# Strassen's scheme for the two projections of a graph-attention layer (stage 0 of a two-layer kernel)

## The chip, the cores and the metric

The kernel runs on one core of one Trainium2 chip. The metric is the device time of one execution in microseconds (us). The five engines of the core are called by their names or by the profile's short forms: TensorE (PE, with its weight loads as PEld), VectorE (DVE), ScalarE (ACT), GpSimd (POOL) and SyncE (SP).

## The reference

Two graph-attention layers run one after the other on 4096 nodes with 512 features in fp32. Only the first layer's projections matter here:

```python
h = jnp.maximum(_layernorm(x, axis=-1), 0.0)      # [4096, 512]
node_att = jax.nn.softmax(h @ node_w, axis=0)     # one logit for each node
he = h @ edge_w                                   # [4096, 512] x [512, 512]
e = jnp.where(adj > 0, he @ he.T, NEG_BIG)
edge_att = jax.nn.softmax(e, axis=1)
support = h @ weight                              # [4096, 512] x [512, 512]
x = x + (adj * (node_att * edge_att)) @ support + bias
```

Stage 0 of the kernel computes the normalised and rectified h, the node logits, `support` (the tile `sup`), the transposed `he` (the tiles `he_t`), and stores x + bias for later. Everything after it (the scores, the attention sums, the second layer) is left as it is by the change.

## The kernel before

The nodes are handled in 32 tiles of 128 rows (t = 0 to 31) and in 8 blocks of 512 rows, four tiles each (b = 0 to 7). The order of all instructions in stage 0 is written out by hand: each engine runs its own queue in the order in which the code names the instructions, and waits on semaphores where data or a buffer is not ready.

What happens to a tile, with the helpers' lines in the kernel before:

- `fetch` (L130) loads 128 rows of x into one of 8 slots `xt`, on SP's queue.
- `stats` (L134) makes mean and variance on VectorE and the square root on ScalarE. `norm` (L142) makes the reciprocal and the shift on VectorE and then h on ScalarE (L149, or L151 for tiles 8 and up, which are written in an order of 32x32 squares).
- `logit` (L153) multiplies h by the node weights with a sum on VectorE (`acc_z`, L154); GpSimd adds the bias into a tile `xb` of its own, of which there is one (L157), and stores it on its own queue (L158).
- `turn` (L176) transposes h. The first 8 tiles go through TensorE (L188) and are copied out of PSUM by VectorE (L189). Later tiles are sent to memory in four pieces (`send`, L160, SP's queue, with the tile's logit), read back in another order (`pull`, L171, SP's queue) and turned in squares by VectorE (L181).

What happens to a block: `support` (L192) multiplies each turned tile by `ws`, in 4 accumulating matmuls of 512 columns into a tile `ps` (two PSUM buffers), which VectorE copies to `sup` (L198). `edges` (L200) makes each 128-row part of `he_t[b]` from `we` and the whole turned block, 4 matmuls of 512 columns into `pe` (two buffers), which ScalarE copies (L205). The loop is L248 to L254: for block b it does the four `edges`, with one `step` (L216) of block b+1 behind each, and then the four `support` of block b+1. A step names, in this order, the fetch of tile t+10 (t+7 early on), the norm and the send of tile t+4, the turn of tile t, the pull of tile t+2 and the stats of tile t+5.

Behind the last block come the maximum of all logits and the softmax over nodes (L257 to L269), alternating between VectorE, GpSimd and ScalarE. Stage 1 (from L289) begins with score tiles of 512, 384, 256 and 128 columns (L331) in six PSUM buffers; ScalarE copies each out (L334) and VectorE masks it and takes maxima (L336 to L344).

Of the kernel before, what the change touches and what calls it, by code (L numbers as in the profile page):

```python
# [8 lines left out]
FP = mybir.dt.float32  # L9
AF = mybir.ActivationFunctionType  # L10
ALU = mybir.AluOpType
AX = mybir.AxisListType
PSUM = bass.MemoryType.PSUM
DRAM = bass.MemoryType.DRAM

P = 128
# [12 lines left out]
def kernel(  # L29
# [15 lines left out]
    nc = tc.nc  # L45
    N, F = x.shape
# [4 lines left out]
    KC = F // P  # L51
    BL = 512
    NB = N // BL
    TB = BL // P
# [27 lines left out]
    sup = big.tile([P, NT, F], FP, name="sup")  # L82
    na = big.tile([P, NT], FP, name="na")
    s_n = big.tile([P, H, NT], FP, name="s_n")
    t_m = big.tile([P, H, NT], FP, name="t_m")
# [10 lines left out]
    he_t = []  # L96
# [3 lines left out]

    with tc.tile_pool(name="w0", bufs=1) as wp, tc.tile_pool(name="a0", bufs=2) as ap_, tc.tile_pool(
        name="a0s", bufs=8
    ) as sp, tc.tile_pool(name="a0p", bufs=2, space=PSUM) as pp, tc.manual_schedule():
        we = wp.tile([P, KC, F], FP, name="we")
        ws = wp.tile([P, KC, F], FP, name="ws")
        nw_b = wp.tile([P, F], FP, name="nw_b")
        nw = wp.tile([P, KC], FP, name="nw")
        bias_b = wp.tile([P, F], FP, name="bias_b")
        nc.sync.dma_start(nw, node_w)
        nc.scalar.dma_start(ws, weight.rearrange("(k p) f -> p k f", p=P))  # L110
        nc.scalar.dma_start(we, edge_w.rearrange("(k p) f -> p k f", p=P))
        nc.gpsimd.dma_start(bias_b, row_bcast(bias, F))

        pw = pp.tile([P, KC, P], FP, name="pt")
        for k in range(KC):
            nc.tensor.matmul(pw[:, k, :], nw[:, k:k + 1].to_broadcast([P, P]), ident, start=True, stop=True)
        nc.vector.tensor_copy(nw_b.rearrange("p (k q) -> p k q", k=KC), pw)
        lg = wp.tile([P, NT], FP, name="lg")
        xts, mvs, sds, hs, hts, hqs = {}, {}, {}, {}, {}, {}
        T0 = 2 * TB  # L120
        nw_s = mb_0

        def squares_of(h):

            return h.rearrange("p (c k q) -> p k c q", c=P // S, q=S)

        def columns_of(x_):
            return x_.rearrange("p (k c q) -> p k c q", k=KC, q=S)

        def fetch(t):  # L130
            xts[t] = sp.tile([P, F], FP, name="xt", bufs=8)
            nc.sync.dma_start(xts[t], x[t * P:(t + 1) * P, :])

        def stats(t):  # L134
            st = sp.tile([P, 6], FP, name="st")
            nc.vector.bn_stats(st, xts[t])
            mvs[t] = sp.tile([P, 2], FP, name="mv")
            nc.vector.bn_aggr(mvs[t], st)
            sds[t] = sp.tile([P, 1], FP, name="sd")
            nc.scalar.activation(sds[t], mvs[t][:, 1:2], AF.Sqrt, bias=eps)  # L140

        def norm(t):  # L142
            rs = sp.tile([P, 1], FP, name="rs")
            nc.vector.reciprocal(rs, sds.pop(t))
            mr = sp.tile([P, 1], FP, name="mr")
            nc.vector.scalar_tensor_tensor(mr, mvs.pop(t)[:, 0:1], -1.0, rs, op0=ALU.mult, op1=ALU.mult)
            hs[t] = sp.tile([P, F], FP, name="h", bufs=5)
            if t < T0:
                nc.scalar.activation(hs[t], xts[t], AF.Relu, bias=mr, scale=rs)  # L149
            else:  # L150
                nc.scalar.activation(squares_of(hs[t]), columns_of(xts[t]), AF.Relu, bias=mr, scale=rs)  # L151

        def logit(t, h):  # L153
            nc.vector.tensor_tensor_reduce(acc_z, h, nw_b if t < T0 else nw_s, 1.0, 0.0, ALU.mult, ALU.add,  # L154
                                           lg[:, t:t + 1])
            xb = sp.tile([P, F], FP, name="xb", bufs=1)
            nc.gpsimd.tensor_tensor(xb, xts.pop(t), bias_b, ALU.add)  # L157
            nc.gpsimd.dma_start(xb_d[t * P:(t + 1) * P, :], xb)  # L158

        def send(t):  # L160


            if t < T0:
                return
            h = hs.pop(t)
            to = h_d[t].rearrange("(c p) (a k q) -> a p c (k q)", p=S, k=KC, q=S)
            for a in range(P // S):
                nc.sync.dma_start(to[a], h[a * S:(a + 1) * S, :].rearrange("p (c f) -> p c f", c=P // S))
            logit(t, h)

        def pull(t):  # L171
            if t >= T0:
                hqs[t] = sp.tile([P, F], FP, name="hq", bufs=2)
                nc.sync.dma_start(hqs[t], h_d[t])

        def turn(t):  # L176
            b, j = divmod(t, TB)
            if j == 0:
                hts[b] = ap_.tile([P, KC, BL], FP, name="h_t")
            if t >= T0:  # L180
                nc.vector.transpose(  # L181
                    hts[b][:, :, j * P:(j + 1) * P].rearrange("p k (a q) -> p k a q", q=S),
                    hqs.pop(t).rearrange("p (a k q) -> p k a q", k=KC, q=S))
                return
            h = hs.pop(t)
            pt = pp.tile([P, KC, P], FP, name="pt")
            for k in range(KC):
                nc.tensor.transpose(pt[:, k, :], h[:, k * P:(k + 1) * P], ident)  # L188
            nc.vector.tensor_copy(hts[b][:, :, j * P:(j + 1) * P], pt)  # L189
            logit(t, h)  # L190

        def support(t):  # L192
            b, j = divmod(t, TB)
            ps = pp.tile([P, F], FP, name="ps")
            for k in range(KC):
                nc.tensor.matmul(ps, hts[b][:, k, j * P:(j + 1) * P], ws[:, k, :],  # L196
                                 start=(k == 0), stop=(k == KC - 1))
            nc.vector.tensor_copy(sup[:, t, :], ps)  # L198

        def edges(b, d):  # L200
            pe = pp.tile([P, BL], FP, name="pe")
            for k in range(KC):
                nc.tensor.matmul(pe, we[:, k, d * P:(d + 1) * P], hts[b][:, k, :],  # L203
                                 start=(k == 0), stop=(k == KC - 1))
            nc.scalar.copy(he_t[b][:, d, :], pe)  # L205

        done = {fetch: 0, stats: 0, norm: 0, send: 0, pull: 0}

        def upto(f, t):
            while done[f] < min(t + 1, NT):
                f(done[f])
                done[f] += 1

        def step(t):  # L216
            if t < NT:
                upto(fetch, t + 10 if t >= T0 else t + 7)
                upto(norm, t + 4)
                upto(send, t + 4)  # L220
                turn(t)
                upto(pull, t + 2)
                upto(stats, t + 5)

        upto(fetch, 7)
        upto(stats, 1)
        upto(norm, 0)
        upto(stats, 2)
        upto(norm, 1)
        turn(0)  # L230
        upto(stats, 3)
        upto(norm, 2)
        turn(1)
        support(0)
        upto(norm, 3)
        turn(2)
        support(1)
        upto(stats, 5)
        upto(norm, 4)
        turn(3)  # L240
        support(2)
        upto(norm, 5)
        support(3)
        upto(fetch, 9)
        upto(stats, 8)
        upto(norm, 7)
        nc.gpsimd.tensor_copy(squares_of(nw_s), columns_of(nw_b))
        for b in range(NB):  # L248
            for j in range(TB):
                edges(b, j)  # L250
                step((b + 1) * TB + j)
            if b + 1 < NB:
                for j in range(TB):
                    support((b + 1) * TB + j)  # L254


        m1 = sp.tile([P, 1], FP, name="m1")  # L257
        nc.vector.tensor_reduce(m1, lg, AX.X, ALU.max)
        m2 = sp.tile([P, 1], FP, name="m2")
        nc.gpsimd.partition_all_reduce(m2, m1, P, bass_isa.ReduceOp.max)  # L260
        m3 = sp.tile([P, 1], FP, name="m3")
        nc.vector.tensor_scalar(m3, m2, -1.0, None, ALU.mult)
        s1 = sp.tile([P, 1], FP, name="s1")
        nc.scalar.activation(na, lg, AF.Exp, bias=m3, accum_out=s1)
        s2 = sp.tile([P, 1], FP, name="s2")
        nc.gpsimd.partition_all_reduce(s2, s1, P, bass_isa.ReduceOp.add)
        s3 = sp.tile([P, 1], FP, name="s3")
        nc.vector.reciprocal(s3, s2)
        nc.vector.tensor_scalar(na, na, s3, None, ALU.mult)  # L269

# [18 lines left out]
    with tc.tile_pool(name="mx", bufs=1) as mxp, tc.tile_pool(name="b_a", bufs=6) as adjp, tc.tile_pool(  # L289
        name="b_e", bufs=4  # L290
    ) as esp, tc.tile_pool(name="b_m", bufs=2) as mkp, tc.tile_pool(name="b_s", bufs=2) as sp, tc.tile_pool(
        name="b_p", bufs=6, space=PSUM
# [56 lines left out]
        for n in range(-6, len(items)):  # L349
# [3 lines left out]
            if n >= 0:  # L353
                i, j, t = items[n]
# [9 lines left out]
    with tc.tile_pool(name="c_a", bufs=11) as adjp, tc.tile_pool(name="c_b", bufs=4) as ebp, tc.tile_pool(  # L364
        name="c_e", bufs=9
    ) as etp, tc.tile_pool(name="c_w", bufs=3) as wkp, tc.tile_pool(name="c_t", bufs=3) as atp, tc.tile_pool(
        name="c_m", bufs=2
    ) as mxp, tc.tile_pool(name="c_o", bufs=4) as iop, tc.tile_pool(name="c_s", bufs=2) as sp, tc.tile_pool(
        name="c_p", bufs=1, space=PSUM
# [754 lines left out]
```

## Time and profile before

| what | value |
|---|---|
| median of 3 runs | 2927.29 us (2926.97 to 2927.95) |
| the profiled execution: its own time | 2927.71 us |
| its span, first to last instruction | 2925.9 us |
| TensorE busy, share of the span | 2880.2 us, 98% |
| VectorE busy | 2539.2 us, 87% |
| ScalarE busy | 1314.6 us, 45% |
| GpSimd busy | 1418.0 us, 48% |
| mean granted TensorE clock | 0.995 |
| stage 0: first transpose to last edge matmul | 12.15 to 241.4 us |

How to read the views that follow. A row of the timeline has the start in us, the length in us, the engine, the line of the kernel, the operation, the tile written and the tiles read, the shape, and how many such instructions were merged. Square brackets hold the idle time of the engine just before, and what ended it. A row of the chain of work has start, length, engine, tile and line, and how many instructions. The length of a matmul row is modelled, and neighbouring matmuls overlap, so the distance between starts tells the pace. A matmul written in the code appears as two instructions (and two weight loads) in the trace.

### The profile page before, as it was taken

The numbers are of one execution on the slowest core, as the hardware profiler recorded it, in microseconds if no ns is written. First come the engines' busy times: TensorE is split into PE (matmuls) and PEld (weight loads), VectorE is DVE, ScalarE is ACT, GpSimd is POOL, SyncE is SP. The second block draws the span as 40 slices with busy tenths as digits, with TensorE's granted clock in tenths as the row PEclk, the third lists the DMA queues.
The fourth block names the chain that finished last, engine by engine and source line by source line (L and its number), as shares of the span: only waits on it lengthen the run. The fifth ranks groups of instructions, "written<-read, shape, count | busy, mean of one in ns | idle before, by whom it ended". The sixth has DMA issues, their size and how long they took to land.

```text
span 2925.9 us, 42903 instructions
## 1 busy us (share of the span) xinstructions
PE 2880.2 (98%) x14987; PEld 1127.2 (39%) x14987; DVE 2539.2 (87%) x3607; ACT 1314.6 (45%) x1798; POOL 1418.0 (48%) x1093
## 2 busy tenths in 40 slices
PE   8999999999999999999999989999999999999998
PEld 4444444444444444444444423322222322222222
DVE  5435777778898998988987789999999999999998
ACT  2221111111122222222221058888777787777786
POOL 3401111112434434444444776676767676767675
PEclk9999999999999999999999989999999999999999
DMA  5525666667877756756655259898989898989896
GB/s 180 176 79 192 224 220 220 228 225 184 201 176 189 204 151 193 195 163 187 196 168 154 69 150 238 236 244 235 242 237 237 239 237 241 233 243 229 218 230 171
DMA packets 517032, 587.66 MB, mean 201 GB/s; under 512 B 291832, under 2 KB 344088, under 8 KB 516816
## 3 DMA queue, kind: packets, MB, share of 16 engines
q1 hardware_dynamic: 460336, 410.90, 46.5%
q0 software_dynamic: 54464, 170.10, 26.1%
q10 hardware_dynamic: 2016, 3.93, 0.4%
q8 instruction: 117, 1.92, 0.3%
q14 instruction: 99, 0.81, 0.1%
HBM read 418.91 MB, written 73.60 MB: 168 GB/s over the span
## 4 chain that ended last, share of the span: by engine, by line
PE 79%; DVE 11%; ACT 4%; issue 4%; DMA 1%; SPq 1%; DVEq 0%; POOL 0%; ACTq 0%; POOLq 0%
PE po L481 27%; PE pv L895 19%; PE pe L331 15%; DVE pr L863 7%; PE dn L900 6%; PE po L592 4%; PE ps L196 3%; PE pe L203 3%; ACT e L827 2%; DVE pr L860 1%; PE pt L954 1%; DVE pt L442 1%; ACT rl L845 1%; DMA eb<-e_d 0%; ACT ex L817 0%
## 5 line engine op out<-in xcount | busy, mean ns | idle before, releaser
L895 PE MATMUL pv<-pr,sup 128*32 128x512 f32 x8192 | 1020.1, 594 | 8.5 <-POOL d_m L1066 5.6
L481 PE MATMUL po<-sup,at 128*128 128x512 f32 x2048 | 883.8, 594 | 7.2 <-DMA eb<-e_d 6.1
L872 POOL TENSOR_TENSOR acc<-acc,pr 128x1024 f32<-128x1024 f32 x240 | 574.0, 2391 | 310.0 <-DVE pr L863 309.4
L863 DVE SCALAR_TENSOR_TENSOR pr<-z,g_m,ex 128x1024 f32<-128x1024 f32 x512 | 630.1, 1270 | 0.0
L481 PEld LDWEIGHTS po<-sup,at 128*128 128x128 f32 x2048 | 388.5, 190 | 494.5 <-issue 454.8
L461 POOL TENSOR_TENSOR racc<-racc,ex 128x512 f32<-128x512 f32 x240 | 352.7, 1469 | 389.3 <-ACT ex L445 387.9
L895 PEld LDWEIGHTS pv<-pr,sup 128*32 128x32 f32 x8192 | 290.6, 110 | 607.3 <-issue 564.7
L445 ACT ACTIVATE ex<-d 128x512 f32<-128x512 f32 x256 | 160.5, 630 | 611.2 <-DVE d L443 605.9
L331 PE MATMUL pe<-he_t,he_t 128*128 128x512 f32 x896 | 386.4, 592 | 0.0
L817 ACT ACTIVATE ex<-e 128x1024 f32<-128x1024 f32 x256 | 263.3, 1028 | 240.9 <-DVE pr L863 239.7
L900 PE MATMUL dn<-pr,d_m 128*2 128x512 f32 x1984 | 343.6, 592 | 0.0
L863 DVE SCALAR_TENSOR_TENSOR pr<-z,g_m,e 128x1024 f32<-128x1024 f32 x256 | 327.8, 1281 | 0.0
L827 ACT ACTIVATE e<-e,ld_m 128x1024 f32<-128x1024 f32 x256 | 290.6, 1135 | 0.0
L860 DVE SCALAR_TENSOR_TENSOR pr<-rl,ngd_m,ex 128x1024 f32<-128x1024 f32 x223 | 283.2, 1270 | 2.1 <-ACT ex L817 1.6
L845 ACT ACTIVATE rl<-z,ngd_m,d_m 128x1024 f32<-128x1024 f32 x223 | 273.9, 1228 | 0.0
L335 POOL DMA_DIRECT2D e_d<-es x144 | 78.7, 546 | 364.5 <-ACT es L334 359.0
L331 PEld LDWEIGHTS pe<-he_t,he_t 128*128 128x128 f32 x896 | 169.2, 190 | 210.1 <-issue 190.8
L334 ACT COPY es<-pe 128x512 f32<-128x512 f32 (+2 forms) x144 | 79.3, 551 | 377.0 <-PE pe L331 377.0
L451 DVE TENSOR_TENSOR at<-ex,a 128x512 f32<-128x512 f32 x256 | 187.3, 732 | 64.6 <-ACT ex L445 38.8
L443 DVE TENSOR_TENSOR d<-pt,mk 128x512 f32<-128x512 f32 x256 | 177.0, 691 | 8.8
L336 DVE CUSTOM_DVE_ANT_0 mk<-pe,mk 128x512 f32<-128x512 f32 (+2 forms) x144 | 93.0, 646 | 98.8 <-ACT es L334 98.7
L878 POOL DMA_DIRECT2D acc<-pr x160 | 138.2, 863 | 5.8 <-DMA acc<-pr 2.8
(183 smaller groups left out, 2539.7 us busy)
## 6 DMA issues: line engine op xcount, KB each, us to landing
e<-in_adj_t_dram SPq DMA_DIRECT2D x256, 512.0 KB, 5.9
acc<-pr POOLq DMA_DIRECT2D x176, 512.0 KB, 5.7
a<-in_adj_t_dram SPq DMA_DIRECT2D x256, 256.0 KB, 4.0
ar<-in_adj_dram SPq DMA_DIRECT2D x120, 256.0 KB, 3.0
e_d<-es POOLq DMA_DIRECT2D x120, 256.0 KB, 3.0
eb<-e_d SPq DMA_DIRECT2D x456, 64.0 KB, 2.9
ac<-in_adj_t_dram SPq DMA_DIRECT2D x112, 256.0 KB, 3.6
et<-e_d SPq DMA_DIRECT2D x112, 256.0 KB, 4.8
```

Source lines behind the costliest of these rows:

```text
L331: nc.tensor.matmul(pe[:, :w], he_t[i][:, k, (t % TB) * P:(t % TB + 1) * P], he_t[j][:, k, BL - w:], start=(k == 0), stop=(k == KC - 1))
L451: nc.vector.tensor_tensor(w, e, aj.pop((b, m)), ALU.mult)
L461: nc.gpsimd.tensor_tensor(racc, racc, e, ALU.add)
L481: nc.tensor.matmul(po[j], w[:, j * P:(j + 1) * P], sup[:, m, :], start=(m == 0), stop=last)
L817: nc.scalar.activation(x_, ra.pop((i, m)), AF.Exp)
L827: nc.scalar.activation(x_, ra[i, m], AF.Exp, bias=ld_m[:, h // HG, m:m + 1])
L845: nc.scalar.activation(r, zs_[i, 0], AF.Relu, bias=ngd_m[:, h // HG, m:m + 1], scale=d_m[:, h, m:m + 1])
L860: nc.vector.scalar_tensor_tensor(w, rl.pop((i, m)), ngd_m[:, h // HG, m:m + 1], x_, op0=ALU.subtract, op1=ALU.mult)
L863: nc.vector.scalar_tensor_tensor(w, zs_[i, k], g_m[:, h + k, m:m + 1], e3.pop((i, m)) if k == 3 else x_, op0=ALU.max, op1=ALU.mult)
L872: nc.gpsimd.tensor_tensor(acc[i, 3], acc[i, 3], w, ALU.add)
L895: nc.tensor.matmul(v[c][q][r * D + c0:r * D + c0 + Q, :], va[:, m, g * HG + k, c0:c0 + Q], pr[i, m, k][:, q * BL:(q + 1) * BL], start=(m = ...
L900: nc.tensor.matmul(dn[r * Q:r * Q + w.shape[1], :], w, src[:, q * BL:(q + 1) * BL], **fl)
```

## The change

Only stage 0 is touched. For blocks 1 to 7 each of the two products (turned block times `ws`, and times `we`) is cut in quarters and made in Strassen's scheme, in Winograd's form with shared sums: seven products of quarters in place of eight. One product of quarters is 4 matmuls in the code, each of 256 columns, and its two halves fill one PSUM bank. Block 0 keeps `support` and `edges`.

- The weights' sums are made once: three tiles for each matrix on GpSimd ahead of block 0's edges (`weight_sums`), and one difference for each in place on VectorE behind block 0 (`last=True`).
- A block's four row sums are made on VectorE right behind the turn of its last tile (`row_sums`), three of them in a `he_t` tile not yet written (for block 7 in `xt` slots), one in place.
- The first product of a set is copied from PSUM by ScalarE; the others are added on VectorE, 7 additions a set, into `sup`, `he_t[b]` or a scratch tile (`parts_of`).
- All of stage 0's PSUM tiles share one name with 8 buffers.
- `xt` has 6 slots rather than 8 and h 4 buffers rather than 5; the bias is added in place in the `xt` slot, so the separate `xb` tile is gone.
- The steps follow the products numbered 3, 6, 9 and 11 of the block's 14. In a step the turn and the row sums come first, then norm, stats, send, fetch and pull. The turns of tiles 6 and 7 come together.

The diff, cut to its core:

```diff
-        name="a0s", bufs=8
-    ) as sp, tc.tile_pool(name="a0p", bufs=2, space=PSUM) as pp, tc.manual_schedule():
+        name="a0s", bufs=8
+    ) as sp, tc.tile_pool(name="a0p", bufs=8, space=PSUM) as pp, tc.manual_schedule():
...
+        XT = 6
...
-            xts[t] = sp.tile([P, F], FP, name="xt", bufs=8)
+            xts[t] = sp.tile([P, F], FP, name="xt", bufs=XT)
...
-            hs[t] = sp.tile([P, F], FP, name="h", bufs=5)
+            hs[t] = sp.tile([P, F], FP, name="h", bufs=4)
...
-            xb = sp.tile([P, F], FP, name="xb", bufs=1)
-            nc.gpsimd.tensor_tensor(xb, xts.pop(t), bias_b, ALU.add)
+            xb = xts.pop(t)
+            nc.gpsimd.tensor_tensor(xb, xb, bias_b, ALU.add)
             nc.gpsimd.dma_start(xb_d[t * P:(t + 1) * P, :], xb)
...
+        def weight_sums(key, w, last=False):
+            B11, B12, B21, B22 = w[:, LO, L], w[:, LO, R], w[:, HI, L], w[:, HI, R]
+            if last:
+                nc.vector.tensor_tensor(B12, B12, B11, ALU.subtract)
+                Ts[key].update({1: B11, 2: B21, 3: B22, 5: B12})
+                return
+            t2, t3 = (wp.tile([P, KC // 2, BL // 2], FP, name=f"{key}t{n}") for n in (2, 3))
+            nc.gpsimd.tensor_tensor(t3, B22, B12, ALU.subtract)
+            nc.gpsimd.tensor_tensor(t2, t3, B11, ALU.add)
+            Ts[key] = {6: t2, 7: t3}
+            if key == "s":
+                t4 = Ts[key][4] = wp.tile([P, KC // 2, BL // 2], FP, name="st4")
+                nc.gpsimd.tensor_tensor(t4, B21, t2, ALU.subtract)
+            else:
+                t4 = Ts[key][4] = [s.rearrange("p h t -> p (h t)") for s in (s_n, t_m)]
+                for k in range(KC // 2):
+                    nc.gpsimd.tensor_tensor(t4[k], B21[:, k, :], t2[:, k, :], ALU.subtract)
+
+        def row_sums(b):
...
+            nc.vector.tensor_tensor(s1, A21, A22, ALU.add)
+            nc.vector.tensor_tensor(s2, s1, A11, ALU.subtract)
+            nc.vector.tensor_tensor(A21, A11, A21, ALU.subtract)
+            nc.vector.tensor_tensor(s4, A12, s2, ALU.subtract)
+            As[b] = {1: A11, 2: A12, 3: s4, 4: A22, 5: s1, 6: s2, 7: A21}
+
+        def product(key, b, n):
+            acc = pp.tile([P, 2, BL // 2], FP, name="bank")
+            A, B = As[b][n], Ts[key][n]
+            for j in range(2):
+                js = slice(j * P, (j + 1) * P)
+                for k in range(KC // 2):
+                    Bk = B[k] if isinstance(B, list) else B[:, k, :]
+                    w, m = (A[:, k, js], Bk) if key == "s" else (Bk[:, js], A[:, k, :])
+                    nc.tensor.matmul(acc[:, j, :], w, m, start=(k == 0), stop=(k == KC // 2 - 1))
+            return acc
...
+            nc.scalar.copy(u, product(key, b, 1))
+            yield
+            add(C[0, 0], u, product(key, b, 2))
+            yield
+            add(u, u, product(key, b, 6))
+            yield
+            add(C[0, 1], u, product(key, b, 5))
+            yield
+            bank = product(key, b, 7)
+            add(C[1, 1], C[0, 1], bank)
+            add(C[1, 0], u, bank)
+            yield
+            add(C[0, 1], C[0, 1], product(key, b, 3))
+            yield
+            add(C[1, 0], C[1, 0], product(key, b, 4))
+            yield
...
-                upto(fetch, t + 10 if t >= T0 else t + 7)
+                if t == T0 - 2:
+                    turn(t)
+                    turn(t + 1)
+                elif t != T0 - 1:
+                    turn(t)
+                if t % TB == TB - 1:
+                    row_sums(t // TB)
                 upto(norm, t + 4)
+                upto(stats, t + 5)
                 upto(send, t + 4)
-                turn(t)
+                upto(fetch, t + 9 if t >= T0 else t + XT)
                 upto(pull, t + 2)
-                upto(stats, t + 5)
...
-        for b in range(NB):
-            for j in range(TB):
-                edges(b, j)
-                step((b + 1) * TB + j)
-            if b + 1 < NB:
-                for j in range(TB):
-                    support((b + 1) * TB + j)
+        weight_sums("s", ws)
+        weight_sums("e", we)
+        for j in range(TB):
+            edges(0, j)
+            step(TB + j)
+        weight_sums("s", ws, last=True)
+        weight_sums("e", we, last=True)
+        for b in range(1, NB):
+            n = 0
+            for key in "se":
+                for _ in parts_of(key, b):
+                    n += 1
+                    if n in (3, 6, 9, 11):
+                        step((b + 1) * TB + (3, 6, 9, 11).index(n))
```

## The prediction

> **What bounds the kernel now.** I read the page first, then stage 0 (from 0 to 242 us) in the chain of work, the timeline and the table by form. The page says which engine the span belongs to:
>
> ```profile
> PE 2880.2 (98%) x14987; PEld 1127.2 (39%) x14987; DVE 2539.2 (87%) x3607; ACT 1314.6 (45%) x1798; POOL 1418.0 (48%) x1093
> ```
>
> An average over the span doesn't price one stage, so the end of the chain inside stage 0 (start, length, work):
>
> ```profile
> 186.42 13.73 PE ps L196 x32
> 200.16 13.73 PE pe L203 x32
> 213.89 13.73 PE ps L196 x32
> 227.62 13.75 PE pe L203 x32
> 241.39 0.59 ACT he_t L205
> 241.99 0.04 issue
> ```
>
> TensorE alone carries it: each block of 512 nodes is 13.73 us of support and 13.73 us of edges, with nothing between. A 4-deep accumulation of 16 matmuls is recorded as 32 instructions, so one record of 512 columns takes 13.73/32 = 0.429 us. The stage after it is TensorE's as well (the L331 records follow at the same 0.43 us), so TensorE time taken out of stage 0 comes off the end.
>
> Two places are not pure work. TensorE waits once for 2.2 us and, at 137.6 us, once for 0.5 us, both times for a support copy that VectorE reaches late:
>
> ```profile
> 54.89 7.13 PE L196 MATMUL ps<-ws,h_t 128*128 128x512 f32 x16 [2.23 <-DVE sup L198]
> ```
>
> Why VectorE is late is visible in pairs of rows of the timeline:
>
> ```profile
> 129.56 1.26 POOL L157 TENSOR_TENSOR xb<-xt,bias_b 128x512 f32<-128x512 f32 x1 [2.64 <-DMA xb_d<-xb]
> 129.68 1.69 DVE L154 CUSTOM_DVE_ANT_0 acc_z<-h,mb 128x512 f32<-128x512 f32 x1 [0.93 <-ACT h L151]
> ...
> 26.10 0.68 DVE L154 CUSTOM_DVE_ANT_0 acc_z<-h,nw_b 128x512 f32<-128x512 f32 x1
> 26.16 1.75 POOL L157 TENSOR_TENSOR xb<-xt,bias_b 128x512 f32<-128x512 f32 x1 [2.85 <-DMA xb_d<-xb]
> ```
>
> Who starts first takes its usual time (1.26 us, 0.68 us); the other is held until it ends.
>
> Last, what a 256-column matmul costs beside its weight load, from the evictions behind score tiles of 384, 256 and 128 columns:
>
> ```profile
> 248.35 0.48 ACT L334 COPY es<-pe 128x384 f32<-128x384 f32 x1 [1.95 <-PE pe L331]
> 250.07 0.37 ACT L334 COPY es<-pe 128x256 f32<-128x256 f32 x1 [1.25 <-PE pe L331]
> 250.97 0.27 ACT L334 COPY es<-pe 128x128 f32<-128x128 f32 x1 [0.52 <-PE pe L331]
> ```
>
> Eight records of 256 columns lie between the first two: 1.72/8 = 0.215 us each, half of 0.429. The 0.190 us weight load stays hidden even there.
>
> **What the Trainium skill says.** *TensorE: Matmul & The Clock Gate*, Back-to-back issue gap: in a stream of weight loads and matmuls both together set the spacing. The trace agrees, with 0.215 us against 0.190 us: at 256 columns the margin is only 25 ns. *SBUF — State Buffer*, Who interferes with whom: VectorE and GpSimd share a port pair that is locked for a whole instruction; a VectorE instruction with two SBUF inputs contends with a GpSimd one that reads SBUF, one with at most one SBUF input doesn't. The pairs above agree with the first half; the second matters for the new additions (one PSUM input, one SBUF input), and no row with GpSimd adding beside them shows it. *PSUM — Partial Sum Buffer*, Specifications: 8 banks of 512 fp32 values, so a product of 2 x 256 fills one bank, and the change takes all 8.
>
> **Part by part.** *Matmuls, blocks 1 to 7.* Removed: 32 x 2 records of 0.429 us, 27.46 us a block. Added: 14 products x 8 records x 0.215 us = 24.08 us. Saved: 3.38 x 7 = 23.7 us, all on the path. Unknown: whether 0.215 us holds for other operands; from 0.2145 (half of 0.429) up to 0.24. I take 0.215.
>
> *The two old stalls.* Support no longer has two buffers of its own but shares 8 banks: 2.2 + 0.5 = 2.7 us more.
>
> *VectorE in a full block (1 to 5).* Start to start: a turned tile 0.63, statistics 0.69 + 0.10, reciprocal and product 0.30, logit 0.62: 2.34 us, four times, 9.4. The sup copies go. New: 14 additions from a bank, at 0.61 us (stage 1's additions from a bank, mean 0.69 us, start 0.60 apart) plus 0.1 where one reads the one before: 9.1. Row sums, 4 at 0.61 plus two such waits: 2.6. Wait for h, about 0.2 a tile since statistics now lie between: 0.8. Sum 21.9 us, under TensorE's 24.08. Bounds of a new operation: 0.60 to 0.75 us (strided results), which gives 21.7 to 24.4. VectorE needn't be on time to the product either: eight banks are 13.8 us of cover, and block b+1's first need of a row sum is its third product, 8.6 us after the step that makes it; turning and two sums take 1.9 us, an addition before it about 1: 5.7 us of slack. If that cover goes, every us of lateness costs one.
>
> *ScalarE.* 28 copies of 0.57 us go, 14 come; it is busy 52 of 241 us: nothing.
>
> *GpSimd.* Each xb addition is now in place, so it waits for h (ScalarE), the moment at which the logit starts too. By the rows above logit starts 0.03 to 0.08 us after h; GpSimd's instructions begin 0.1 to 0.3 us after what they wait for. So VectorE should win, and GpSimd be held (1.75 us), which costs nothing: 4 x (1.75 + 0.3 + 0.56) = 10.4 us of 24. If GpSimd wins, VectorE pays about 1.2 us a tile (rival 2). New weight sums: five of 128x512 and two halves at 1.26 to 1.75 us with 0.3 between, about 10 us, from 24 to 34 us, ahead of xb(4) on GpSimd's queue.
>
> *SP and the x tiles, where I expect a new stall.* There are 6 slots, not 8, and one is free only when its xb store has landed (median 3.0 us). So fetch(10) waits for xb(4): added at 34 to 35.3, store issued 35.6, landed 38.6; on SP it stands behind send(8), issued 38.8, landed (4.0 us) 42.8. VectorE's step 5 reaches stats(10) at 39.5 and waits 3.3 us. Fetch(11) waits for xb(5) and lands at 48.5, about when wanted; the logits of tiles 6 and 7 meet xb(6) and xb(7), 0.5 and 1.0 us; fetch(12), behind send(10), is issued at 51.0 and lands at 55.2. Step 7 makes block 1's second row sum by 51.3, then waits from 53 to 55.2 for stats(12), and behind that, the logit and this queue stand the last weight sums: ws is ready at 57.2. TensorE is through block 0 at 45.6 and wants the row sum after two products (49.0) and that weight sum after three: it waits 2.3 + 4.1 = 6.4 us. Bounds: none, if stores land a us sooner each and VectorE is never held, to 10 us if each link is 1 us later. I take 6.4. Later fetches run five tiles ahead and pulls have 8.6 us or more (landing 3.1 us, four sends and a fetch at 0.44 each before them): hidden.
>
> *The end of stage 0.* The logit maximum, the exponential and the release of stage 1's loads now stand behind VectorE's last addition rather than a support copy 13.7 us earlier. Before, TensorE's end to the first load was 3.4 us, with a table load of 1.28 us in it that no longer has to wait for the last copy; the new chain is longer by two hops. I make it equal, 0 to 2 us later. Stage 1's first six tiles, 15.4 us, need no release (bank 0 was freed 6 us early): nothing.
>
> **Sum.** 23.7 + 2.7 - 6.4 = 20.0 us. The profiled execution took 2927.71 us (span 2925.9 and 1.8 around it); 2927.71 - 20.0 = 2907.7. The runs' median is 0.4 us lower, so I say 2907.5. Change under 0.2% (5.9 us) can't be told from none here.
>
> **Rivals.** (1) No start-up stall: stores at startup land in 2.3 us and SP is early; 26 us gained, 2901. For it: TensorE has 15 us of block 0 to cover; against: three waits in series on SP.
> (2) GpSimd takes the port first at every tile. VectorE needs 21.9 + 4 x 1.2 = 26.7 us a block, 2.6 over TensorE, 13 over five blocks; less 5.7 of slack, 7.4 us lost: 2915. For it: in two pairs of rows a lead of 0.12 us or less settled it; against: GpSimd's later start.
> (3) Slower: weight loads surface. At 256 columns only 25 ns separate matmul and load; 7 x 14 x 8 = 784 records, so 20.0/784 = 26 ns more each cancels everything. At 50 ns (a quarter of a load uncovered) 39 us: 2947. Against it: the eight records at 0.215 us; for it: they reused one operand for both sides, and a product here waits for a bank and for a sum.
>
> **How the numbers follow.** Forecast 0.58 (2903 to 2912), rival 1 0.15 (2900 to 2903), rival 2 0.17 (2912 to 2920), rival 3 0.07; 0.03 for a loss to about no change. The range 2900 to 2919 leaves out some 0.12. Faster 0.88, same 0.05, slower 0.07.
>
> **What would show it.** Products 1.72 us apart in blocks 2 to 7 (24.1 us a block): the saving. TensorE idle about 6 us between 47 and 58 us, released by VectorE, with VectorE waiting for xt: the stall. Logits at 0.69 us with xb additions stretched: VectorE won; logits over 1.2 us and TensorE waiting for VectorE at each third product: rival 2. Records above 0.24 us apart: rival 3, and I'm wrong in sign. Stage 0 should end near 221 us.

## The result, and the profile after

The changed kernel takes 2912.97 us in the median (2912.11 to 2913.22, five runs), the kernel before in the same comparison 2926.97 us (2925.47 to 2927.95): a ratio of 0.995 with a 95% interval of 0.9939 to 0.9961, 14.0 us or 0.48% faster. The forecast was 2907.5 us in a range of 2900 to 2919. The profiled execution took 2913.0 us, with a span of 2911.2 us.

The page's line of busy times, as before: TensorE is still the engine of the span.

```profile
PE 2863.5 (98%) x15323; PEld 1194.0 (41%) x15323; DVE 2601.3 (89%) x3707; ACT 1307.9 (45%) x1784; POOL 1439.7 (49%) x1100
```

The chain of work at the end of stage 0 (start, length, work) holds one unbroken piece of products and then stage 1:

```profile
60.28 166.36 PE bank L265 x760
226.64 0.02 issue
226.66 0.69 DVE he_t L286
227.36 0.10 DVE m L372
227.46 0.04 issue
227.50 17.88 PE pe L445 x53
```

Stage 1 begins at 227.50 us; before it was 242.03. These 14.5 us are the whole change of the span (14.7): what was gained in stage 0 came off the end.

In the steady part the forecast's pace holds. TensorE's rows of the timeline (start, length, then line, tiles, shape), for the same product in blocks 2, 3 and 4:

```profile
84.88 1.89 PE L265 MATMUL bank<-st,he_t 128*128 128x256 f32 x8
...
109.05 1.89 PE L265 MATMUL bank<-st,he_t 128*128 128x256 f32 x8
...
133.22 1.89 PE L265 MATMUL bank<-st,he_t 128*128 128x256 f32 x8
```

From start to start a block takes 24.17 us (forecast 24.08, before 27.46), 0.216 us a record. What differs lies before 67 us. TensorE's rows there:

```profile
48.32 3.62 PE L265 MATMUL bank<-ws,h_t 128*128 128x256 f32 x16
55.46 3.75 PE L265 MATMUL bank<-st,he_t 128*128 128x256 f32 x8 [3.52 <-DVE he_t L250]
60.28 3.75 PE L265 MATMUL bank<-ws,he_t 128*128 128x256 f32 x8 [1.08 <-DVE ws L224]
63.83 2.22 PE L265 MATMUL bank<-st,h_t 128*128 128x256 f32 x8
65.88 1.89 PE L265 MATMUL bank<-ws,he_t 128*128 128x256 f32 x8
```

Two waits, for the second row sum (L250) and for the support weights' last sum (L224), at the places where the forecast had them. But the two products behind them take 3.5 us each and not 1.73. The table of windows (window, busy time and records, granted clock, DMA share, GB/s) says why: TensorE's granted clock was halved there.

```profile
54.00:64.00 10.00, 7.47 (x17) 0.51 0.67 197
```

And VectorE and GpSimd in the same stretch of the timeline:

```profile
47.01 1.28 POOL L159 TENSOR_TENSOR xt<-xt,bias_b 128x512 f32<-128x512 f32 x1
47.22 1.63 DVE L156 CUSTOM_DVE_ANT_0 acc_z<-h,nw_b 128x512 f32<-128x512 f32 x1
...
49.17 1.28 POOL L159 TENSOR_TENSOR xt<-xt,bias_b 128x512 f32<-128x512 f32 x1
49.39 1.63 DVE L156 CUSTOM_DVE_ANT_0 acc_z<-h,nw_b 128x512 f32<-128x512 f32 x1
...
52.28 1.75 POOL L159 TENSOR_TENSOR xt<-xt,bias_b 128x512 f32<-128x512 f32 x1 [0.97 <-ACT h L153]
...
52.84 1.75 DVE L249 TENSOR_TENSOR he_t<-h_t 128x512 f32<-128x512 f32 x1
```

GpSimd's additions stand in its queue in the order of the logits. Those of tiles 8 and 9 wait there for their h (until 39.54 and 44.87 us); those of tiles 5, 6 and 7, whose h had long been ready, follow right behind. Each of these three begins 0.2 us ahead of its logit, and the logit takes 1.63 us in place of 0.68. Freed, VectorE needs one turn (0.6 us) to its next logit and GpSimd a pause and a store (0.3 + 0.56 us) to its next addition, so they meet again at once. Even the row sum is held, 1.75 us for 0.69. From 40 to 54.6 us five logits and this sum take 5.0 us more than the same instructions do when nothing holds them. From 40 to 60 us VectorE is busy 18.26 of 20 us and waits for x only 1.4 us.

### The profile page after: what moved, and what is told of

The parts are those of the page before. It is cut to its first block, busy times and chain, and to the rows that moved or that the text cites. A ratio compares the mean times of both kernels' runs of the same rounds, so it can differ in the third digit from the quotient of the medians.

```text
span 2911.2 us, 43773 instructions
## 1 busy us (share of the span) xinstructions
PE 2863.5 (98%) x15323; PEld 1194.0 (41%) x15323; DVE 2601.3 (89%) x3707; ACT 1307.9 (45%) x1784; POOL 1439.7 (49%) x1100
## 4 chain that ended last, share of the span: by engine, by line
PE 89%; DVE 5%; issue 2%; DMA 1%; ACT 1%; SPq 1%; POOL 0%; DVEq 0%; ACTq 0%; POOLq 0%
PE po L595 28%; PE pv L1009 27%; PE pe L445 15%; PE dn L1014 8%; PE bank L265 6%; PE po L706 4%; DVE pr L977 3%; PE pt L1068 1%; DVE pt L556 1%; DMA xt<-in_x_dram 1%; ACT e L941 1%; PE bank L198 0%; SPq L523 0%; DVE at L565 0%; DVE mk L550 0%
```

## The experiments

The theory after this profile: VectorE reaches block 1's row sums and the last weight sum late because GpSimd's additions hold it (the shared port pair that the prediction named), and TensorE's pause then halves its clock. The rival is the reason in the prediction: fetches of x that wait for a free slot. All were timed beside the kernel before, whose median was 2927.45 us for the first four kernels, 2927.86 for the next four, 2927.93 for the last three (2926.97 for the changed kernel); between these groups, a difference of a us says nothing.

**Without the bias addition.** The line of the addition is left out, and with it the bias in the result.

```diff
-            nc.gpsimd.tensor_tensor(xb, xb, bias_b, ALU.add)
```

> The changed kernel without GpSimd's bias addition (x is stored as it is; the bias is left out of the result). GpSimd then has no addition in stage 0 but the weight sums. Theory (port): in block 0 VectorE is held by GpSimd's additions for some 5.7 us between 40 and 60 us and the reciprocal's follow-up at 12.5 us for 0.8 us; without them the pauses of TensorE before blocks 1's third and fourth product (3.5 and 1.1 us) shrink under 1 us together, the half clock behind them (3.6 us) goes, and the start is 1 to 2 us earlier: 2902 to 2905 us. Rival (x slots, the reason given in the prediction): the pauses come from statistics that wait for x; slots are freed only about 1.5 us sooner here, so 2909 to 2912 us.

2905.03 us (ratio 0.9921, 0.9908 to 0.9935), 8 us under the changed kernel. Logits take 0.69 us throughout, the row sum comes at 49.1 us, and the third product follows the second without a wait. One pause stays:

```profile
54.19 2.81 PE L264 MATMUL bank<-ws,he_t 128*128 128x256 f32 x8 [2.73 <-DVE ws L223]
```

The clock was halved in this one too, which the theory had not expected. Behind VectorE's lateness there stood, this time, 1.4 us of waiting for x at 51.9 us. Some 2.2 of the 8 us are gained before block 1 begins (46.12 us rather than 48.32). The holds are the larger cause, and x is next in line.

**Sums early.** Block 1's row sums and the support weights' last sum stand right behind the turn of tile 7.

```diff
                     turn(t)
                     turn(t + 1)
+                    row_sums(1)
+                    weight_sums("s", ws, last=True)
...
-                if t % TB == TB - 1:
+                if t % TB == TB - 1 and t != T0 - 1:
...
-        weight_sums("s", ws, last=True)
```

> The changed kernel with block 1's row sums and the last sum of the support weights named right behind the turn of tile 7, ahead of that step's norm, statistics and logit; nothing is added or left out. Theory (VectorE's order and speed in block 0 cause the pauses): the second row sum is ready near 52.3 us rather than 55.3, the weight sum near 54.2 rather than 60.2; TensorE pauses under 1 us in all, its clock is not halved, about 3.8 + 3.6 us are gained: 2905 to 2907 us. Rival (only the pauses matter, the halved clock has another cause): 3.8 us gained, about 2909 us, with the clock still halved between 55 and 64 us.

2910.59 us (0.9941, 0.9928 to 0.9953): the forecast of this run missed by 4 us. Block 1 is as expected: the third product at 51.34 us after a wait of 0.55 us, the clock whole, although the logits are held as before (1.62 us). So in the kernel as changed two things come together: the holds, and row sums that stand in VectorE's queue behind another tile's norm, statistics and logit. But the pause is only put off by a block:

```profile
80.70 3.75 PE L265 MATMUL bank<-st,he_t 128*128 128x256 f32 x8 [4.87 <-DVE he_t L250]
```

VectorE's rows show what made it late there:

```profile
59.10 0.69 DVE L138 BATCH_NORM_STATS2 st<-xt 128x6 f32<-128x512 f32 x1 [3.07 <-DMA xt<-in_x_dram]
...
74.50 0.71 DVE L183 STREAM_TRANSPOSE h_t<-hq 128x512 f32<-128x512 f32 x1 [2.02 <-DMA hq<-h_d]
```

Part of the gain was given back later, to two waits for transfers.

**Keep TensorE busy in the pauses.**

```diff
+        def fill(n):
+            acc = pp.tile([P, BL], FP, name="bank")
+            for k in range(n):
+                nc.tensor.matmul(acc, ws[:, k, 0:P], hts[0][:, k, :], start=(k == 0), stop=(k == n - 1))
...
+            if b == 1 and key == "s":
+                fill(4)
             add(u, u, product(key, b, 6))
             yield
+            if b == 1 and key == "s":
+                fill(3)
             add(C[0, 1], u, product(key, b, 5))
```

The results of these matmuls are read by nobody.

> The changed kernel with matmuls whose results nobody reads put into TensorE's two pauses in block 1 (4 of 512 columns ahead of the third product, 3 ahead of the fourth). The third and fourth product still start when VectorE lets them, at 55.5 and 60.3 us. Theory (the pause itself halves TensorE's granted clock): products three and four take 1.73 us rather than 3.5 us; only the fourth's gain shows at the end, 1.8 us: 2910.5 to 2911.5 us, and a granted clock of 1.0 between 54 and 64 us. Rival (the clock is halved by something else, or the long records come from waiting): no gain, 2913 us or a little over, the clock still at 0.5 there.

2910.24 us (0.9939, 0.9927 to 0.9952), 2.7 us less with more work. The same window as above:

```profile
54.00:64.00 10.00, 9.63 (x37) 1.00 0.64 186
```

The products behind the pauses begin at 54.76 and 59.59 us and take their usual time. So the pause halves the clock. Some 0.7 us of the gain is not the clock: in this execution block 1 already began 0.7 us earlier, at 47.63 us, with the same instructions up to there.

**The kernel before with the new order of a step and 8 shared PSUM buffers.** The new names and the number of the PSUM tiles are cut here.

```diff
-                upto(fetch, t + 10 if t >= T0 else t + 7)
+                turn(t)
                 upto(norm, t + 4)
+                upto(stats, t + 5)
                 upto(send, t + 4)
-                turn(t)
+                upto(fetch, t + 10 if t >= T0 else t + 7)
                 upto(pull, t + 2)
-                upto(stats, t + 5)
```

> The kernel before with two parts of the change alone: stage 0's PSUM tiles share 8 buffers, and a step names turn, norm, statistics, send, fetch, pull in this order. No Strassen scheme, no in-place bias addition, x slots as before. Theory: the two old waits of TensorE for a late support copy (2.2 and 0.5 us) go, nothing else moves: 2924 to 2925 us. Rival (those waits have another cause and come back elsewhere): 2927 us.

2925.19 us (0.9991, 0.9983 to 0.9999): 2.3 us, at the edge of what can be measured; stage 1 starts at 239.51 us rather than 242.03, and TensorE waits for no support copy any more. Block 1 began 0.8 us later in this execution (46.41 us rather than 45.63), so the two old waits were worth 3.3 us from there on.

**Bias apart, x slots, and both with the sums early.** Four kernels ask whether slots matter. In the first, whose edit comes first below, GpSimd writes the biased row to an unused row of `sup`, so it doesn't wait for h and a slot is free sooner; in the third, x of tiles 0 to 11 is loaded into such rows, so that no fetch waits for a slot before tile 18. The second and fourth add the sums' early place.

```diff
-            xb = xts.pop(t)
-            nc.gpsimd.tensor_tensor(xb, xb, bias_b, ALU.add)
+            xb = sup[:, (t + 24) % NT if t < T0 else t, :]
+            nc.gpsimd.tensor_tensor(xb, xts.pop(t), bias_b, ALU.add)
```

```diff
-            xts[t] = sp.tile([P, F], FP, name="xt", bufs=XT)
+            xts[t] = sup[:, NT - 12 + t, :] if t < 12 else sp.tile([P, F], FP, name="xt", bufs=XT)
```

> The changed kernel with the biased row written to a row of the support tile that is not in use yet, rather than in place: GpSimd's addition then waits for x alone and not for h, and an x slot is free when the addition has run, about 4 us before the store lands. Order and all else as changed. Theory (port holds in block 0 and x slots both matter): the hold of 0.8 us at 12.5 us goes and the start is 2 us earlier; fetches are earlier, holds stay: pauses 3 to 4 us in all: 2908 to 2911 us. Rival A (x slots alone): pauses gone, 2903 us. Rival B (port alone): as changed but for the start, 2911 us.

> As e5 with e2's order (block 1's row sums and the support weights' last sum right behind the turn of tile 7). Theory: e2 lost its gain in block 1, where VectorE waited 3.1 + 0.6 us for x and 2.0 us for a pulled tile and so came 4.9 us late to block 2's row sum; with slots freed earlier these waits shrink below what the 5.7 us of slack cover: no pause over 1 us in any block, no half clock: 2902 to 2905 us. Rival (VectorE is short of time in block 1 by its own work): a pause in block 2 of 3 us or more again, 2908 to 2910 us.

> The changed kernel with the x of tiles 0 to 11 loaded into rows of the support tile not in use yet, so that no fetch in blocks 0 and 1 waits for a slot; the bias is still added in place, and the order is as changed. Theory (port and slots): VectorE's waits for x go (0.9 + 0.4 us between 44 and 58 us), the holds by GpSimd stay (5 to 6 us), so the pause before the third product stays 2 to 3.5 us and the clock is halved: 2910 to 2912.5 us. Rival (x slots alone, as the prediction had it): pauses gone, 2904 us.

> As e8 with e2's order. Theory: no waits for x in block 1, so block 2's row sum is in time and TensorE doesn't pause over 1 us after block 0: 2904 to 2906 us. Rival (VectorE short of time by its own work): a pause in block 2 again, 2909 us or more.

Measured: 2912.97 (0.9947, 0.9934 to 0.9959), 2912.73 (0.9948, 0.9936 to 0.9961), 2912.00 (0.9945, 0.9933 to 0.9958) and 2911.24 us (0.9943, 0.993 to 0.9957): within 2 us of the changed kernel, all four. The third settles the rival: without any slot to wait for, TensorE's waits are what they were, by its table of waits (engine, tile and line, releaser, us, times, longest):

```profile
PE bank L265 <- DVE he_t L250: 3.5, 1, 3.5
PE bank L265 <- DVE ws L224: 1.1, 1, 1.1
```

The slots cause nothing that is seen at the end. My own forecasts for the first, second and fourth fell too. In the first, the additions no longer wait for h and meet VectorE at other moments: its `mr` of two tiles is held to 1.32 us at 11.15 and 1.25 us at 13.37, and block 1 begins only 0.5 us earlier (47.81 us), not 2. In the second and fourth, with the sums early, TensorE paused 7.6 and 4.2 us at block 2's row sum, though slots were free sooner or not needed. In the fourth, VectorE still waited until 59.77 us, 3.07 us, for tile 12's x. SP's rows of that kernel name the reason; the fetch at 56.65 us is tile 12's:

```profile
54.85 1.75 SPq L170 DMA_DIRECT2D h_d<-h  x4
56.65 0.45 SPq L134 DMA_DIRECT2D xt<-in_x_dram  x1
...
65.04 1.77 SPq L170 DMA_DIRECT2D h_d<-h  x4
66.85 1.96 SPq L134 DMA_DIRECT2D xt<-in_x_dram  x4
68.91 0.42 SPq L176 DMA_DIRECT2D hq<-h_d  x1
```

The fetch stands behind a send, the send waits for h, and h comes from VectorE's own norm of that step: one chain around the loop, in which no slot has a part. Then a pull stands behind four fetches.

**Fetches ahead.** To the fourth of these kernels one line is added ahead of block 0's loop, so that x of tiles 0 to 17 is named ahead of every send.

```diff
+        upto(fetch, 17)
         nc.gpsimd.tensor_copy(squares_of(nw_s), columns_of(nw_b))
```

> As e9 (x of tiles 0 to 11 in rows of the support tile, sums early), and the fetches of tiles 0 to 17 are all named ahead of block 0's loop, so that none stands behind a send on SP's queue. Bias in place at the logit as changed. Theory (a fetch named behind a send, which waits for h, is what makes VectorE wait for x once the order is tightened): no wait for x in blocks 0 and 1, pulls no longer behind four fetches, block 2's row sum in time, no pause over 1 us and no half clock after block 0: 2903 to 2906 us. Rival (GpSimd's holds leave VectorE short of time anyway): a pause of 3 us or more in block 2 again, 2909 us or more.

2905.82 us (0.9922, 0.991 to 0.9934), as the theory had it, 5.4 us under the fourth. VectorE waits for no x, the longest wait of TensorE for a row sum is 1.2 us, the clock is whole; and GpSimd still holds logits for up to 1.63 us. So what the fourth kernel lost in block 2 was lost to the order on SP's queue and not to VectorE's own work.

**The bias later.** The additions of tiles 0 to 11 leave blocks 0 and 1 for the steps 20 to 31, in blocks 4 to 6; x waits in `sup`'s rows until then, and the fetches of tiles 0 to 17 stand ahead as in the kernel just shown (both cut here). Nothing is left out.

```diff
+            if t >= 12:
+                biased(t)
+
+        def biased(t):
             xb = xts.pop(t)
...
                 upto(pull, t + 2)
+                if t >= NT - 12:
+                    biased(t - (NT - 12))
```

> The changed kernel with x of tiles 0 to 11 in rows of the support tile, the fetches of tiles 0 to 17 ahead, and the bias additions of tiles 0 to 11 moved out of blocks 0 and 1 to the steps of blocks 4 to 6 (nothing left out); the order of the sums as changed. Theory (GpSimd's additions beside block 0 hold VectorE): as without the bias, row sum ready near 49.6 us, and with no wait for x also the weight sum by 52 us: pauses under 1.5 us, clock whole: 2901 to 2904 us. Rival (additions only move their holds to later blocks): pauses there, 2908 us or more.

> e11 with e2's order as well. Theory: nothing left for it to cure beyond some 1 us: 2900 to 2903 us, no pause of TensorE over 0.5 us from the first edge matmul to stage 1. Rival: the earlier sums push norm and statistics back, so that a pulled tile or a row sum of block 2 is late: 2904 us or more.

2903.23 us (0.9914, 0.9901 to 0.9928) with the sums where the change put them, 2901.36 us (0.9909, 0.9894 to 0.9924) with the sums early. The second differs from the kernel with the fetches ahead (2905.82 us) in the place of the additions alone: 4.5 us. In the first, TensorE's only wait in the products is 0.5 us; in the second there is none, and stage 1 starts at 216.70 us:

```profile
46.45 3.62 PE L269 MATMUL bank<-ws,h_t 128*128 128x256 f32 x16
49.90 1.89 PE L269 MATMUL bank<-st,he_t 128*128 128x256 f32 x8
51.63 1.89 PE L269 MATMUL bank<-ws,he_t 128*128 128x256 f32 x8
```

This last kernel beats both: 26.6 us under the kernel before and some 11.6 us under the changed one. Stage 1 starts 25.3 us earlier than before (242.03 - 216.70); the scheme's 23.0 us and the two old waits' 3.3, less 0.8 by which block 1 begins later (46.45 us against 45.63), come to 25.5. TensorE's rows are back to back from the first edge matmul on.

## Why the prediction was right, and what in it was wrong

Right in sign and in the main term, inside the range, 5.5 us too fast at its point. The number lies just inside the bracket that the prediction had kept for its rival 2, GpSimd taking the port first (2912 to 2920 us). That is also what happened, but in block 0 alone and not at every tile. (The sum has a slip that changes nothing: 2907.7 less 0.4 is 2907.3, not 2907.5.)

- *Matmuls, 23.7 us.* Measured (27.46 - 24.17) x 7 = 23.0 us. The record takes 0.216 us, not 0.215; the weight load stays hidden, also where weights and moving tile differ and each product waits for a bank (rival 3 falls).
- *The two old stalls, 2.7 us.* Measured 3.3 us by the kernel before in the new order, counted from the start of block 1: by the distances of TensorE's rows, the two waits took some tenths more than 2.2 and 0.5 us.
- *VectorE in a full block, 21.9 us.* In the window from 78 to 102 us it is busy 20.57 us; additions from a bank take 0.69 us each, also beside GpSimd's additions. TensorE waits for VectorE nowhere from block 2 on.
- *GpSimd against the logit.* In the steady blocks VectorE came first each time, as forecast: 20 logits of 0.691 to 0.694 us, GpSimd held to 1.77 us. The lead is small (63.92 against 63.98 us for the first of them). In block 0 it was the other way round, which the step named only for tiles 6 and 7: it took h to release logit and addition together, but in block 0 VectorE comes to its logits later than that.
- *The new stall, 6.4 us: the size was right by luck and the cause wrong.* The fourth product starts at 60.28 us; with no wait it would have started after three products of 1.73 us from 48.32, at 53.5: 6.8 us late. TensorE waited for 3.5 + 1.1 us of it; the rest is the long third product. I had written "SP and the x tiles, where I expect a new stall". The kernel without slots leaves it as it was; the one without bias additions takes most of it away, and so does the one that keeps them and moves them later (with x in `sup` and the fetches ahead): GpSimd's holds, on logits and on the row sum itself, are what makes VectorE late in the order of the change. With the sums early the same holds cost TensorE 0.55 us in block 1. The prediction had the pair of rows that shows such a hold in its first part, and priced 1.5 us of it.
- *Not in the prediction at all: the clock.* Of the two long products the first is covered (TensorE would have waited for the weight sum until 60.28 anyway); the second, and the start of the next, cost 1.8 + 0.3 = 2.1 us. The Trainium skill has this, in *TensorE: Matmul & The Clock Gate*, What's actually happening: an idle TensorE falls to half its clock and needs some 3.4 us of work to come back. That section puts the idle time at about 3.4 us; here 2.73 us were enough (last section). I had read the granted clock of 1.0 and not asked what a pause of 6 us does to it.
- *Not in the prediction: the start.* TensorE is through with block 0's edges at 48.3 us, before at 45.6: 2.7 us. The in-place addition waits for h, and so falls on the second tile's norm:

```profile
12.12 1.27 POOL L159 TENSOR_TENSOR xt<-xt,bias_b 128x512 f32<-128x512 f32 x1 [9.43 <-ACT h L151]
...
12.46 0.95 DVE L148 SCALAR_TENSOR_TENSOR mr<-mv,rs 128x1 f32<-128x1 f32 x1
```

The second transpose starts 0.7 us later than before, and the first support tile takes longer. The chain of work has both, after and before:

```profile
14.30 1.12 PE bank L190 x4
15.42 5.83 PE bank L198 x8
...
13.58 1.11 PE pt L188 x4
14.69 4.44 PE ps L196 x8
```

The tile's first records run at half pace for longer (though the table of windows gives a granted clock of 1.00 there). Why is open. The pause of TensorE ahead of it, 1.1 us, doesn't explain it: with the same instructions and the same pause the tile took 4.44 us in the kernel with the sums early and 5.07 with TensorE kept busy. These two begin block 1 at 47.17 and 47.63 us, so between 1.5 and 2.7 us of start are lost from one execution to another; without bias additions in block 0 it is 0.5 to 0.9 us.

Together: 23.0 + 3.3 - 6.8 - 2.1 - 2.7 = 14.7 us, against 14.5 us at the start of stage 1, which follows the last product by 0.9 us rather than 0.6. Of the forecast's error of 5.5 us, 4.8 us are the clock and the start, the two terms that were missing, as this execution had them.

## What to carry to other kernels

When a scheme takes work off TensorE and puts sums on VectorE, price the transition into it as well as the steady state: there the new sums wait behind everything that the slower engines have queued. If GpSimd works beside VectorE, look for pairs of rows in which one is held, and count every instruction of VectorE with two SBUF inputs in the stretch where GpSimd has additions queued. A long pause of TensorE (here 2.7 us and more) is to be charged twice: for itself, and for the half clock behind it; and curing one wait shows the next, so look at the block after.

## What the runs showed of the hardware

A pause of 2.23 us between products left TensorE's clock whole (the kernel before, at 52.6 us); one of 2.73 us (without the bias addition) and one of 3.03 us (bias apart) were followed by a halved clock, as were the longer ones in block 1 and 2 of the other kernels (3.5 to 7.6 us). The table of windows for TensorE, first the kernel before, then the one without the bias addition (window, busy time and records, granted clock):

```profile
54.00:56.00 2.00, 1.11 (x3) 1.00 0.31 17
56.00:58.00 2.00, 2.00 (x7) 1.00 0.88 310
...
54.00:56.00 2.00, 1.81 (x7) 0.79 0.91 276
56.00:58.00 2.00, 2.00 (x6) 0.50 0.29 114
```

In the second the clock fell about 1 us after work had begun again. Worked out from windows of 1 us, the stretch at half clock lasted 3.4 us in two kernels (without the bias addition; the fourth of the slot kernels), 6.8 us in three (sums early; the first and second of the slot kernels) and 10.2 us in two (the changed kernel and the third of the slot kernels, each with a second pause in between). From the end of the last pause it took 3 to 5 us of work until the clock was whole: with the sums early the products from 80.70 us take 3.54 and 2.52 us, and the next the usual 1.73.

VectorE's additions of a PSUM bank and an SBUF tile kept their 0.68 to 0.69 us in all 98 cases with GpSimd adding beside them part of the time, while instructions with two SBUF tiles were held for up to 1.06 us in the changed kernel, and a logit for 1.5 us with the bias apart (2.17 us at 15.15).
